# Four graph layers on one core: the comparison of a transposed block of adjacency comes two steps behind its transfer, with five buffers instead of four

## The chip, the cores and the metric

The kernel runs on one core of one Trainium2 chip. The metric is the device time of one execution in microseconds (us). The kernel before takes 3604.29 us, the median of three runs (3601.26 to 3607.97). The engines named below are TensorE (PE, with its weight loads as PEld), VectorE (DVE), ScalarE (ACT), GpSimd (POOL) and SyncE (SP), whose queue only issues transfers here.

## What is computed

Four layers run over 3327 nodes with 512 features; `adj` is a dense 3327 x 3327 matrix of int32 zeros and ones, shared by all layers. Layers 0, 1 and 2 are graph attention with 8, 4 and 8 heads, layer 3 is a mean over neighbours. Layer 0, cut to what matters:

```python
h = jnp.maximum(_layernorm(x, axis=-1), 0.0)
Wh = jnp.einsum('nd,hdo->hno', h, W)
e = jax.nn.leaky_relu(f1[:, :, None] + f2[:, None, :], negative_slope=ALPHA)
e = jnp.where(adj[None, :, :] > 0, e, NEG_INF)
attention = jax.nn.softmax(e, axis=-1)
h_prime = jnp.einsum('hnm,hmo->hno', attention, Wh)
x = x + elu(h_prime)
```

The product over neighbours wants adjacency with the neighbour on the partitions, so each 128 x 128 tile of `adj` must be transposed and turned into a mask of 0 and 2 in one-byte numbers.

## The kernel before

**Tiling.** The 3327 nodes are 26 tiles of 128. Rows are taken in 7 chunks of up to four tiles (`chunks`); columns in five groups of 6, 6, 6, 4 and 4 tiles (`JG`). `attention` (L678) runs over the chunks, within a chunk over the heads, within a head over two passes of two row tiles each. For every pair of row tile and column tile PE does two matmuls, one with `tht` (L760) and one with `gt` (L763). These two are made per column group by `matrices` (L646): four or six comparisons per group on ACT (L664) or DVE (L661), then on DVE an `and` with the mask (L668) and an `xor` (L670). There are seven buffers each of `tht` and `gt`, against five groups per head, so DVE and ACT can be little more than one group into the next head before PE has used the current one. At the end of a pass DVE sums the accumulators (`R`, L778), and at the end of a head it scales the result (L796 to L803).

**Where masks come from.** The masks of chunk 0 are made ahead of the loop with transposes on PE. Those of the other chunks are made during layer 0, 110 blocks (22 row tiles x 5 groups), by `mask_steps` (L212). Each block has three stages: `load` issues the transfer of `adj` to a tile `at` from POOL (L226; three buffers); `turn` issues from SP a transposing transfer of `at` into a tile `tr` (L238; four buffers); `compare` turns `tr` into `st` on DVE (L245), takes the diagonal tile where the block holds it (`d`, L250, and `dg`, L251; 22 blocks of the 110) and stores `st` to DRAM from SP (L252). `mask_tiles` (L261) loads the masks of a chunk back (L265).

**How the stages are staggered.** `in_steps` (L889) lays the blocks out as a pipeline: step `i` runs the last stage of block `i - s`, then the one before, down to the first stage of block `i`. With three stages there are 112 steps, and a comparison is in the step right after the one that issued its transposing transfer. `Hooks.run` (L602) is called after every pass (the "hook") and takes one step, or two on some hooks: on every odd one in chunk 0, and on every third in the chunks after it. So in a hook with two steps the transfer and its comparison can stand in the same hook. Before the last head of a chunk a loop (L808) takes further steps until the masks of the next chunk are done.

**What sets the order.** The program text is reordered by a scheduler, which puts each instruction on its engine's queue where it judges it ready; the queue itself is then in order. `after(inst, name)` holds an instruction behind a named one in that judgement: `load`, `turn` and the L245 comparison are held behind the last matmul of the pass (`gone[-1]`). `d` (L250) has no such hold.

The buffers of layer 0 are laid out by `tags` (L943): there `R` takes 4 x 2 x 129 floats per partition, while its layer-0 use is 4 x 2 x 65.

Of the kernel before, what the change touches and what calls it, by code (L numbers as in the profile page):

```python
# [25 lines left out]
F32 = mybir.dt.float32  # L26
BF16 = mybir.dt.bfloat16
# [10 lines left out]
P = 128  # L38
# [14 lines left out]
def tile_gnn(ctx: ExitStack, tc: tile.TileContext, x, adj, W0, a01, W1, al, ar, W2, a2,  # L53
# [7 lines left out]
    def pn(t):  # L61
        return min(P, N - t * P)

    PER = 4
# [3 lines left out]
    JM = max(n for _, n in JG)  # L68
# [76 lines left out]
    def after(inst, name):  # L145

        tc.add_manual_dep(inst.ins, name, mybir.DependencyInfo(mybir.DependencyClass.NoSync,
                                                               mybir.DependencyReason.SCHED_ONLY))
# [62 lines left out]
    def mask_steps(pool, t, g):  # L211


        n = pn(t)
        c, k = where[t]
        j0, nj = JG[g]
        w = min(nj * P, N - j0 * P)
        q = {}

        def load():  # L220
            at = q["at"] = pool.tile([P, JM * P], BF16, name="at", bufs=3)
            if n < P:
                nc.vector.memset(at, 0.0)
            elif w < nj * P:
                nc.vector.memset(at[:, w:nj * P], 0.0)
            ld = nc.gpsimd.dma_start(at[:n, :w], adj[t * P:t * P + n, j0 * P:j0 * P + w])  # L226
            after(ld, gone[-1] if gone else stored[NT - 1] if c else relus[-3])

        def turn():
            at = q["at"]  # L230
            if c == 0:
                tp = q["tp"] = ps.tile([P, 8, P], BF16, name="tp", bufs=2)
                for j in range(nj):
                    nc.tensor.transpose(tp[:, j, :], at[:, j * P:(j + 1) * P], identb)
                compare()
            else:
                tp = q["tp"] = mp.tile([P, JM, P], BF16, name="tr", bufs=4)
                tr = nc.sync.dma_start(tp[:, :nj], at[:, :nj * P], transpose=True)  # L238
                after(tr, gone[-1] if gone else stored[NT - 1])

        def compare():
            hooks.done += 1
            tp = q["tp"]
            st = masks0[g][:, k] if c == 0 else pool.tile([P, JM, P], FP8, name="st", bufs=3)[:, :nj]
            cm = nc.vector.tensor_scalar(st, tp[:, :nj], 0.0, 2.0, op0=ALU.is_gt, op1=ALU.mult, saturate=False)  # L245
            if gone:
                after(cm, gone[-1])
            if j0 <= t < j0 + nj:
                d = pool.tile([P, P], BF16, name="d", bufs=1)
                nc.vector.tensor_tensor(d, tp[:, t - j0, :], negI, ALU.is_gt)  # L250
                nc.vector.tensor_scalar(dg1[:, t, :], d, 2.0, None, op0=ALU.mult, saturate=False)  # L251
            nc.sync.dma_start(maskd[c][g][:, k], st)  # L252
        return (load, turn) if c == 0 else (load, turn, compare)

    def mask_view(c, g):
        nt, nj = chunks[c][1], JG[g][1]
# [635 lines left out]
    with tc.tile_pool(name="first", bufs=1) as fp:  # L892
# [21 lines left out]
        order = [(t, g) for g in range(len(JG)) for t in range(PER)]  # L914
        order += [(t, g) for t in range(PER, NT) for g in range(len(JG))]
        hooks.masks = in_steps([mask_steps(ip, t, g) for t, g in order[:20]])
        hooks.tiles = [node_stages(L, t, lambda lead=1, t=t: first_x(t, lead), fp, True) for t in range(NT)]
        folds, hooks.small = hooks.small, []
# [21 lines left out]
        while hooks.small:  # L940
            hooks.small.pop(0)()
    A, R = [("A", D, F32, n) for n in A_BUFS], ("R", PER * 2 * 129, F32, 1)
    ab, gt, tht = ("ab", JM * 400, BF16, 7), ("gt", PER * JM * P, FP8, 7), ("tht", PER * JM * P, FP8, 7)  # L943
    tags = [[A[0], R, tht, ("tr", JM * P, BF16, 4), ("abx", 4 * 400, BF16, 4), gt],
            [A[1], ("ab", JM * 258, F32R, 7), R, ("ts", 2 * JM * P, F32R, 3), ("tv", 2 * 4 * P, F32R, 2), tht[:3] + (10,)],
            [A[2], ab, ("R", PER * 2 * 65, F32, 1), tht, gt]]
    hooks.masks = in_steps([mask_steps(ip, t, g) for t, g in order[20:]])
    for l in range(3):
        att = ExitStack()
        if l == 2:  # L950
            yp = main.enter_context(tc.tile_pool(name="early", bufs=1, side="right", reuse_waits="tile"))
        mp = att.enter_context(tc.tile_pool(name=f"att{l}", bufs=1, reuse_waits="tile"))
# [526 lines left out]
```

## Time and profile before

| | before |
|---|---|
| median of three runs | 3604.29 us |
| the profiled execution's own time | 3600.56 us |
| its span, first to last instruction | 3598.7 us |
| mean granted TensorE clock | 0.986 |
| PE busy in the span | 3457.0 us (96%) |
| DVE busy | 2619.6 us (73%) |
| ACT busy | 2508.1 us (70%) |
| transposing transfers (L238) | 110, issued from 187.9 to 997.5 us, 5.4 us median from issue to landing (2.9 to 10.8) |
| L245 on `tr` | 110, from 196.7 to 1010.2 us, 550 ns median |
| L250 on `tr` | 22, from 197.2 to 1004.3 us, 291 ns median |

The blocks of this change are made between about 190 and 1010 us of the span. "Idle before" in a row of the timeline is how long an engine stood still ahead of the instruction, with the engine or transfer whose semaphore released it.

### The profile page before, as it was taken

How to read it: one execution, taken by the hardware profiler on the slowest of the kernel's cores; microseconds unless marked ns; L12 is line 12 of the kernel's file. 1: busy time of each engine (PE TensorE's matmuls, PEld its weight loads, DVE VectorE, ACT ScalarE, POOL GpSimd, SP SyncE). 2: the span in 40 equal slices, each digit the busy share in tenths (PEclk: the TensorE clock that was granted, in tenths of full speed). 3: DMA queues.
4: the chain of work that ended last, by engine and by line, in shares of the span. 5: the costliest groups of instructions: out<-in, count | busy, mean ns of one | idle time of the engine just before them, and what ended most of it. 6: DMA issues, size and time to landing. Idle time of an engine off the chain costs nothing. (4 is left out here: it accounts for less than half of the span.)

```text
span 3598.7 us, 77661 instructions
## 1 busy us (share of the span) xinstructions
PE 3457.0 (96%) x30751; PEld 3114.2 (87%) x30751; DVE 2619.6 (73%) x5227; ACT 2508.1 (70%) x4113; POOL 620.4 (17%) x858
## 2 busy tenths in 40 slices
PE   7888999999999999999999989999999999999998
PEld 6778999999999878888888869989898989877887
DVE  7777778888887779898888868877676767672221
ACT  5766787777787888888888767766676667572111
POOL 6600222111110211232223230101010101010000
PEclk9999999999999999999999999999999999999999
DMA  7698899999966877777777886655555555576331
GB/s 212 217 257 209 220 255 231 248 250 256 241 214 211 299 251 288 263 266 281 276 254 272 298 289 216 196 169 174 179 193 173 183 177 179 167 266 260 118 103 56
DMA packets 398120, 797.72 MB, mean 222 GB/s; under 512 B 112969, under 2 KB 221844, under 8 KB 397104
## 3 DMA queue, kind: packets, MB, share of 16 engines
q1 hardware_dynamic: 363890, 723.14, 62.6%
q0 software_dynamic: 28128, 62.42, 7.6%
q10 hardware_dynamic: 5726, 7.08, 0.6%
q8 instruction: 245, 4.01, 0.5%
q14 instruction: 131, 1.07, 0.1%
HBM read 663.59 MB, written 129.64 MB: 220 GB/s over the span
## 5 line engine op out<-in xcount | busy, mean ns | idle before, releaser
L664 ACT ACTIVATE gt<-s1b,ks 128x512 fp8e4<-128x512 f32 (+1 forms) x2448 | 1448.0, 677 | 291.5 <-issue 175.8
L760 PE MATMUL acc<-ab,tht 128*128 128x195 bf16 (+1 forms) x9112 | 1559.6, 249 | 10.1 <-DVE tht L668 9.3
L763 PE MATMUL acc<-ab,gt 128*128 128x195 bf16 (+1 forms) x9112 | 1558.5, 249 | 7.2 <-DVE gt L670 3.6
L763 PEld LDWEIGHTS <-gt 128*128 128x128 fp8e4 x10744 | 1056.4, 98 | 60.1 <-issue 44.4
L760 PEld LDWEIGHTS <-tht 128*128 128x128 fp8e4 x10744 | 1055.7, 98 | 41.8 <-DVE tht L668 28.1
L668 DVE TENSOR_TENSOR tht<-gt,m 128x768 uint32<-128x768 uint32 (+3 forms) x557 | 446.5, 802 | 118.4 <-ACT gt L664 116.8
L670 DVE TENSOR_TENSOR gt<-tht,m 128x768 uint32<-128x768 uint32 (+3 forms) x557 | 449.5, 807 | 8.7
L633 ACT CAST ts<-tht 128x1536 fp32r<-128x1536 fp8e4 x208 | 300.0, 1469 | 58.6 <-PE acc L753 54.9
L753 PE MATMUL acc<-ab,ts 128*128 128x258 f32 x2496 | 332.3, 289 | 5.5 <-DMA ab<-ab 3.4
L753 PEld LDWEIGHTS acc<-ab,ts 128*128 128x128 f32 x2496 | 312.0, 189 | 15.0 <-issue 3.7
L763 PE MATMUL acc<-abx,gt 128*128 128x195 bf16 (+1 forms) x1632 | 289.4, 250 | 27.1 <-DVE rc L800 15.4
L661 DVE TENSOR_SCALAR gt<-s1b,ns 128x512 fp8e4<-128x512 f32 (+1 forms) x446 | 216.0, 490 | 131.2 <-PE acc L763 130.4
L664 ACT ACTIVATE tht<-s1b,ks 128x512 fp8e4<-128x512 f32 (+1 forms) x504 | 308.3, 679 | 3.0 <-DMA s1b<-s 2.5
L1015 PE MATMUL acc<-y,mf 128*128 128x512 f32 x1352 | 309.8, 391 | 0.5 <-DVE mf L1010 0.5
L760 PE MATMUL acc<-abx,tht 128*128 128x195 bf16 (+1 forms) x1632 | 290.2, 250 | 14.4 <-DVE tht L668 11.3
L1015 PEld LDWEIGHTS acc<-y,mf 128*128 128x128 f32 x1352 | 253.5, 188 | 56.6 <-DVE mf L1010 0.9
L863 POOL TENSOR_TENSOR xt<-xt,e 128x512 f32<-128x512 f32 x72 | 126.1, 1752 | 913.8 <-DVE e L862 595.5
L778 DVE TENSOR_REDUCE R<-acc 128x130 f32<-128x390 f32 x416 | 214.5, 555 | 77.5 <-PE acc L763 76.8
L756 PE MATMUL acc<-ab,tht 128*128 128x387 bf16 x1248 | 227.3, 331 | 8.5 <-DMA ab<-ab 4.7
L1012 ACT CAST mf<-m 128x768 fp32r<-128x768 fp8e4 (+1 forms) x78 | 59.1, 762 | 243.9 <-PE acc L1015 232.1
L753 PE MATMUL acc<-ab,tv 128*128 128x258 f32 x1664 | 219.1, 283 | 2.3 <-DVE tv L633 1.5
L753 PEld LDWEIGHTS acc<-ab,tv 128*128 128x128 f32 x1664 | 207.1, 189 | 4.3 <-DVE tv L633 2.7
(163 smaller groups left out, 3709.1 us busy)
## 6 DMA issues: line engine op xcount, KB each, us to landing
ab<-ab SPq DMA_DIRECT2D x333, 600.0 KB, 5.3
ab<-ab SPq DMA_DIRECT2D x112, 774.0 KB, 6.4
ab<-ab SPq DMA_DIRECT2D x112, 516.0 KB, 5.4
ab<-ab SPq DMA_DIRECT2D x112, 400.0 KB, 3.9
abx<-ab SPq DMA_DIRECT2D x110, 400.0 KB, 7.3
ab<-ab SPq DMA_DIRECT2D x56, 582.0 KB, 7.1
s1b<-s SPq DMA_DIRECT2D x120, 256.0 KB, 6.1
m<-mask SPq DMA_DIRECT2D x69, 384.0 KB, 4.1
```

The costliest lines, as they stand in the source:

```text
L633: (nc.scalar.copy if KIND[g] == "s" else nc.vector.tensor_copy)(t[:, :k1 - k0, :nj], th[a][g][:, k0:k1])
L661: nc.vector.tensor_scalar(gv[:, :, jj, :], s1v, L.ns2[:, j, h:h + 1], 2.0, op0=ALU.is_gt, op1=ALU.mult, saturate=False)
L664: nc.scalar.activation(gv[:, :, jj, :], s1v, AF.Relu, bias=L.ks2[:, j, h:h + 1], scale=BIG, saturate=False)
L668: nc.vector.tensor_tensor(pu, gu, mu, ALU.bitwise_and)
L670: nc.vector.tensor_tensor(gu, pu, mu, ALU.bitwise_xor)
L753: mm = nc.tensor.matmul(acc[k][:, :2 * DA], thr[g][:, k - ks[0], jj, :], ab[a][g][:, jj, :], start=(j == 0), stop=(j == NT - 1), skip_grou ...
L756: mm = nc.tensor.matmul(acc[k][:, :3 * DA], th[a][g][:, k, jj, :], ab[a][g][:, jj, :3 * DA], start=(j == 0), stop=(j == NT - 1), skip_grou ...
L760: nc.tensor.matmul(acc[k][:, :3 * DA + o], th[0][g][:, k, jj, :], ab[0][g][:, jj, :3 * DA + o], start=(j == 0), stop=False, skip_group_che ...
L763: mm = nc.tensor.matmul(acc[k][:, AO:AO + 3 * DA + o], th[1][g][:, k, jj, :], ab[0][g][:, jj, AO:AO + 3 * DA + o], start=False, stop=(j == ...
L778: nc.vector.tensor_reduce(R[:, k], v.rearrange("p a (s d) -> p a d s", s=3), AX.X, ALU.add)
L863: nc.gpsimd.tensor_add(xt, xt, e)
L1015: nc.tensor.matmul(acc[k], mf[:, jj, :], y2[g][:, jj, s, :], start=(j0 + jj == 0 and s == 0), stop=(j0 + jj == NT - 1 and s == 1))
```

## The change

A fourth stage that does nothing is put between `turn` and `compare`, so a comparison comes two steps behind the issue of its transposing transfer; there are 113 steps instead of 112. `tr` gets a fifth buffer (1536 bytes per partition), and the reservation of `R` in layer 0 shrinks from 129 to 65 floats (2048 bytes per partition less). No instruction is added or removed.

```diff
-                tp = q["tp"] = mp.tile([P, JM, P], BF16, name="tr", bufs=4)
+                tp = q["tp"] = mp.tile([P, JM, P], BF16, name="tr", bufs=5)
                 tr = nc.sync.dma_start(tp[:, :nj], at[:, :nj * P], transpose=True)
...
-        return (load, turn) if c == 0 else (load, turn, compare)
+
+        return (load, turn) if c == 0 else (load, turn, lambda: None, compare)
...
-    tags = [[A[0], R, tht, ("tr", JM * P, BF16, 4), ("abx", 4 * 400, BF16, 4), gt],
+    tags = [[A[0], ("R", PER * 2 * 65, F32, 1), tht, ("tr", JM * P, BF16, 5), ("abx", 4 * 400, BF16, 4), gt],
```

## The prediction, made before the changed kernel ran

> **What bounds the kernel now.** I began with the page: PE is busy for 96% of the span, so time is won only where PE stands still or is slow. Busy time by stretch then shows where that is, for the stage in which masks are made:
>
> ```profile
> 190.00:340.00 150.00, 128.85 (x1409) 124.40 (x1410) 113.42 (x233) 102.54 (x168) 12.52 (x23) 0.94 0.94 232
> 340.00:600.00 260.00, 243.24 (x2645) 236.85 (x2643) 204.07 (x414) 199.97 (x339) 58.73 (x83) 0.96 0.93 226
> 600.00:1010.00 410.00, 398.03 (x4388) 388.86 (x4386) 334.14 (x703) 321.90 (x547) 68.18 (x102) 1.00 1.00 255
> ```
>
> The columns are the stretch, its length, busy us (and instructions) of PE, PEld, DVE, ACT and POOL, then the granted TensorE clock, the DMA share and GB/s. PE is idle for 21.2 + 16.8 + 12.0 = 49.9 us of these 820 us. It also runs at a reduced clock: 0.06 x 150 + 0.04 x 260 = 19 us of full clock are missing. DVE is busy for 651.6 us (79%), so on average it has room. The list of waits, cut to 180 to 1015 us, says who stops it:
>
> ```profile
> DVE st L245 <- DMA tr<-at: 75.7, 26, 7.7
> DVE d L250 <- DMA tr<-at: 38.7, 14, 6.6
> DVE tht L668 <- ACT gt L664: 24.1, 29, 2.5
> ...
> PE acc L760 <- DVE tht L668: 17.2, 15, 3.1
> PE acc L763 <- DVE rc L800: 15.4, 11, 6.4
> PE acc L763 <- DVE gt L670: 8.9, 8, 2.4
> PE acc L763 <- DVE rc L801: 4.8, 3, 3.7
> PE acc L760 <- DMA mask<-st: 3.1, 1, 3.1
> ```
>
> (Total us, times, longest.) DVE stands 114.4 us for transposed blocks that have not landed; PE stands for DVE. The timeline joins the two:
>
> ```profile
> 390.57 0.68 DVE L668 TENSOR_TENSOR tht<-gt,m 128x512 uint32<-128x512 uint32 x1
> 391.17 0.69 DVE L796 TENSOR_TENSOR R<-R,cpm 128x520 f32<-128x520 f32 x1
> ...
> 396.89 0.43 DVE L245 TENSOR_SCALAR st<-tr 128x512 fp8e4<-128x512 bf16 x1 [5.02 <-DMA tr<-at]
> 397.23 0.42 DVE L798 TENSOR_TENSOR R<-R 128x260 f32<-128x260 f32 x1
> 397.57 0.69 DVE L670 TENSOR_TENSOR gt<-tht,m 128x512 uint32<-128x512 uint32 x1
> 398.17 0.16 DVE L800 TENSOR_SCALAR rc<-R 128x4 f32<-128x4 f32 x1
> 398.25 0.95 DVE L668 TENSOR_TENSOR tht<-gt,m 128x768 uint32<-128x768 uint32 x1
> 398.40 0.32 PE L763 MATMUL acc<-abx,gt 128*128 128x195 bf16 x1 [6.40 <-DVE rc L800]
> ```
>
> The head's last `gt` (L670) stands behind the comparison. The comparison is held 5.02 us by its transfer, and PE, whose next matmul needs that `gt`, stands 6.40 us. (The releaser named is `rc`; the missing operand is the `gt` that ends just then.)
>
> **What the Trainium skill says.** "Perfetto Trace Analysis", Tensor Engine Instruction, calls ACT, DVE and GpSimd strict FIFO; the rows above agree, L798 and L670 start only once L245 has. "DMA: Bandwidth & Descriptors", Rules for kernel authors, says to issue a transfer early, compute, and wait for its semaphore late, which is the form of this change. "TensorE: Matmul & The Clock Gate", Part 1, says the clock halves after an idle window of about 3.4 us and returns after about 3.4 us of work. Here it agrees: the 10 us from 394, from 536 and from 327 us were granted 0.66, which is 6.8 us at half rate each.
>
> **The change, part by part.** (1) *The waits of L245.* I set each idle stretch of PE over 0.25 us between 180 and 1015 us beside DVE's last wait before it in the timeline: 42 stretches, 52.6 us. About 37 us follow a wait of L245 for `tr`; 5.5 us follow such a wait at 327 us, where the loop at L808 takes extra steps; 4.6 us follow a wait of L250; 4.0 us are the first passes before 194 us; 1.5 us have no such cause. One pass is about 10 us (19.7 us per head), and one step more puts at least one pass between the issue of a transfer and its comparison, where the two now can share a hook. Landing takes 5.4 us in the median and 10.8 at most, so nearly all of the 26 waits go. Not all of PE's 37 us go with them: the stretches of 0.4 to 0.8 us at head ends stand behind DVE's own chain of sums. I take 30 us.
>
> (2) *The clock.* Half-rate stretches follow L245 waits at 266, 352, 394 (two), 588 and 896 us: with grants of 0.83, 0.83, 0.66, 0.83 and 0.83 over 10 us that is 1.7 + 1.7 + 3.4 + 1.7 + 1.7 = 10.2 us of clock. PE stood still in part of it. I take 9 us.
>
> (3) *The diagonal `d`.* The order of the built kernel shows what the text doesn't: `d` is not held behind the pass, so the scheduler still puts it where it thinks the transfer has landed, and that does not move by a step. Before, 17 of the 22 `d` stand ahead of their L245; after, all 22 do, by 10 to 33 instructions. So the 14 waits (38.7 us) stay and up to 8 come new, each like those there are, 2.8 us: some 22 us more of DVE standing. What that costs PE is small as long as DVE is ahead: of the 14 waits only three are followed by idle PE, 4.6 us in all, plus 3.4 us of clock at 536 us; that is 0.6 us per `d`. Eight more are 5 us. If none of the new ones is felt it is 0; at the size of the one at 536 us (2.9 us idle and 3.4 of clock) all eight would be 50 us.
>
> (4) *The loop at L808, and the queues.* At the end of chunk 0 the loop takes two steps instead of one, so the comparisons of blocks 18 and 19 still stand in the same hook as the issue of their transfers: the 5.5 us and 3.4 us of clock at 327 us stay. On SP, the load of chunk 1's second mask group now stands behind the store of block 18 and two more transposes, where before it was issued at 315.7 us; by the DVE order it is wanted at about 332 us. With the store at about 328 us and 4.1 us for a mask load it comes 0 to 2 us late. With one more comparison of 0.55 us in that hook I take 1.5 us. Later chunks need no extra steps (42 blocks are compared by the step where 40 are needed).
>
> (5) *The rest.* SP's transposes stay one step behind the loads, so POOL's wait for `at` (234.2 us on `tr`) is as before and hides behind its idle time. Five `tr` buffers leave the same three steps of reuse as four did. The order of matmuls differs only within the first head, and the order after 1010 us not at all. `R` and `tr` shift addresses; I put that at 0, with 3 us either way for a wait at the start of layer 1 (2.8 us of PE at 1350 us now).
>
> DMA share is 0.93 to 1.00 in this stage, but in 940 to 1020 us PE was busy throughout beside a share of about 1, so a PE without gaps can be fed.
>
> Sum: 30 + 9 - 5 - 1.5 = 32.5, so the profiled time goes from 3600.56 to 3568. The runs' median lies 3.7 us above the profiled time, which gives 3571.8; I say 3571.
>
> **The rivals.** *A, the sum above:* 3571, own range 3548 to 3590. The upper end is (1) and (2) in full, the 8.9 us of (4) won too and no `d` felt anew: 37 + 10.2 + 8.9 = 56 us; the lower one is 14 us, a third of (1) and (2).
>
> *B, the wait moves to `d`.* DVE still stands for `tr`, in 22 places instead of 40, and these come where it is just in time. For it: the order of the built kernel. Against it: eleven of the 14 waits at `d` cost PE nothing. If half of the gain is given back, 3604 - 16 = 3588.
>
> *C, nothing shows:* transfers are the true limit, the blocks land later as PE gets faster, and the gaps return at `ab` or the masks. For it: the share of 1.00. Against it: PE waits for a transfer once in the stage, 3.1 us. 3604, within 0.2%.
>
> *D, slower:* the same place as B at full price. `d` stands between `tht` and `gt` of a group, and all 22 hold the group that PE wants next. At 6 us of waiting with 2.5 us felt and 1.2 us of clock, 22 x 3.7 = 81, less the 8 there are now, against 39 + 1.5 won or lost elsewhere: 3604 + 73 - 37.5 = 3640. The point from which it decides is 2.1 us felt per `d`: (37.5 + 8) / 22. Mildly past it, at 2.6 us, 3616.
>
> **How the numbers follow.** A 0.62, B 0.15, C 0.08, D 0.15. A run of this kernel can be told from no change at about 0.2%, 7 us. Faster is A and B and a little of C: 0.78; same 0.07; slower 0.15. The range that leaves 2 in 10 out reaches from A's upper savings through B to just below no change: 3546 to 3598.
>
> **What would show it.** Waits of L245 for `tr` fall from 75.7 us to under 15; those of L250 stay or rise to 40 to 70 us; PE's idle time in the stage falls from 50 us to about 20; the grant rises to 0.97 or more in 190 to 340 us; the stage ends near 977 us instead of 1010, with nothing changed behind it. The wait at the end of chunk 0 (327 us, earlier by what is won before it) stays. Wrong would be: idle time of PE behind L250 as large as what L245 gave up, or PE waiting for masks or `ab`.

## The result, and the profile after

The changed kernel takes 3561.08 us, the median of four runs (3554.17 to 3569.33), beside 3605.22 us for the kernel before (four runs). The ratio is 0.9879, 95% interval 0.9855 to 0.9903, so it is faster by 35 to 52 us, 1.2%. The profiled execution took 3569.33 us (the slowest of the four) with a span of 3567.4 us, 31.3 us less than before; the kernel before was profiled at 3600.56 us, under its own median. From L254 on, the line numbers of the changed kernel are one higher: L669 is the `and` (L668 before), L671 the `xor`, L761 and L764 the matmuls, L801 and L802 the `rc` rows.

Busy time by stretch, changed kernel, with the columns of before (length, then busy us of PE, PEld, DVE, ACT, POOL, granted clock, DMA share, GB/s):

```profile
190.00:340.00 150.00, 142.32 (x1606) 140.16 (x1607) 125.71 (x259) 113.55 (x185) 16.50 (x29) 0.95 1.02 255
340.00:600.00 260.00, 249.36 (x2731) 243.10 (x2729) 212.04 (x426) 206.92 (x352) 61.98 (x86) 0.98 0.99 239
600.00:980.00 380.00, 373.37 (x4132) 365.94 (x4130) 317.86 (x663) 303.20 (x516) 62.99 (x95) 1.00 1.01 257
```

PE's idle time in the stage is 7.7 + 10.6 + 6.6 = 24.9 us where it was 49.9, and the missing clock 0.05 x 150 + 0.02 x 260 = 12.7 us where it was 19.4. That is 32 us together. The instructions of the stage are the same; in its first 150 us PE got through 1606 matmuls instead of 1409.

The list of waits of the changed kernel, 180 to 985 us (total us, times, longest):

```profile
DVE d L250 <- DMA tr<-at: 53.1, 17, 7.7
DVE tht L669 <- ACT gt L665: 34.4, 40, 2.5
...
DVE tht L669 <- DMA tr<-at: 5.3, 1, 5.3
DVE st L245 <- DMA tr<-at: 3.9, 1, 3.9
...
DVE tht L669 <- DMA m<-mask: 2.2, 1, 2.2
...
PE acc L761 <- DVE tht L669: 16.2, 10, 3.2
PE acc L764 <- DVE gt L671: 4.2, 4, 1.4
PE acc L764 <- DVE rc L801: 3.8, 5, 0.8
```

The comparison L245 waits once instead of 26 times. `d` waits more than before (53.1 us, it was 38.7), and 40 short waits for ACT instead of 29 fit a DVE that is less often late and now meets operands that ACT has not made yet. All instructions on the blocks, as the view of one tile gives them:

```profile
L238 SPq DMA_TRANSPOSE tr<-at x110: 1188/1274/3857, 184.9 to 958.8; - x110
L245 DVE TENSOR_SCALAR st<-tr x110: 392/551/1631, 202.2 to 977.6; 128x768 fp8e4<-128x768 bf16 x66, 128x512 fp8e4<-128x512 bf16 x44
...
DMA to landing us min/median/max: 2.4/5.2/10.7
```

The transfers are as slow to land as before (5.2 us in the median, 5.4 before); they are only waited for later. The last comparison starts at 977.6 us instead of 1010.2, and from there to the end of the span it is 2589.8 us, where it was 2588.5. Everything won in this profile is won in this stage.

### The profile page after: what moved, and what is told of

Same layout as the page of the kernel before. It is cut to its first block, busy times and chain, and to the rows that moved or that the text cites. A ratio compares the mean times of both kernels' runs of the same rounds, so it can differ in the third digit from the quotient of the medians.

```text
span 3567.4 us, 77669 instructions
## 1 busy us (share of the span) xinstructions
PE 3450.4 (97%) x30751; PEld 3112.8 (87%) x30751; DVE 2626.8 (74%) x5227; ACT 2507.5 (70%) x4113; POOL 626.2 (18%) x858
## 5 line engine op out<-in xcount | busy, mean ns | idle before, releaser
L761 PE MATMUL acc<-ab,tht 128*128 128x195 bf16 (+1 forms) x9112 | 1556.3, 248 | 6.1 <-DVE tht L669 5.3
L764 PE MATMUL acc<-ab,gt 128*128 128x195 bf16 (+1 forms) x9112 | 1555.2, 248 | 5.8 <-DVE rc L801 3.3
L764 PEld LDWEIGHTS <-gt 128*128 128x128 fp8e4 x10744 | 1055.2, 98 | 38.1 <-issue 25.8
L761 PEld LDWEIGHTS <-tht 128*128 128x128 fp8e4 x10744 | 1054.6, 98 | 36.9 <-DVE tht L669 23.3
L669 DVE TENSOR_TENSOR tht<-gt,m 128x768 uint32<-128x768 uint32 (+3 forms) x557 | 448.1, 805 | 136.9 <-ACT gt L665 127.7
L671 DVE TENSOR_TENSOR gt<-tht,m 128x768 uint32<-128x768 uint32 (+3 forms) x557 | 449.9, 808 | 8.5
L761 PE MATMUL acc<-abx,tht 128*128 128x195 bf16 (+1 forms) x1632 | 289.0, 250 | 15.0 <-DVE tht L669 14.8
L764 PE MATMUL acc<-abx,gt 128*128 128x195 bf16 (+1 forms) x1632 | 288.5, 250 | 8.4 <-DVE rc L801 3.8
```

Of the source, the lines that this page charges most:

```text
L669: nc.vector.tensor_tensor(pu, gu, mu, ALU.bitwise_and)
L671: nc.vector.tensor_tensor(gu, pu, mu, ALU.bitwise_xor)
L761: nc.tensor.matmul(acc[k][:, :3 * DA + o], th[0][g][:, k, jj, :], ab[0][g][:, jj, :3 * DA + o], start=(j == 0), stop=False, skip_group_che ...
L764: mm = nc.tensor.matmul(acc[k][:, AO:AO + 3 * DA + o], th[1][g][:, k, jj, :], ab[0][g][:, jj, AO:AO + 3 * DA + o], start=False, stop=(j == ...
```

## The experiments

Each ratio is to the kernel before, run on the same chip as the experiment. Times in us of different sets are not compared directly: the kernel before has medians of 3605.22, 3599.46, 3596.66 and 3598.05 us in the four sets.

### Which part of the change does it: e1 and e2

e1 has the empty stage alone, e2 the buffers alone.

```diff
 e1
-        return (load, turn) if c == 0 else (load, turn, compare)
+        return (load, turn) if c == 0 else (load, turn, lambda: None, compare)
 e2
-                tp = q["tp"] = mp.tile([P, JM, P], BF16, name="tr", bufs=4)
+                tp = q["tp"] = mp.tile([P, JM, P], BF16, name="tr", bufs=5)
...
-    tags = [[A[0], R, tht, ("tr", JM * P, BF16, 4),
+    tags = [[A[0], ("R", PER * 2 * 65, F32, 1), tht, ("tr", JM * P, BF16, 5),
```

> The empty stage alone: four buffers for tr, R reserved as before. Its instructions stand in the same order on every engine as in the changed kernel. Theory (the step of distance makes the gain): as the changed kernel, 3553 to 3570 us, waits of L245 for tr under 10 us, idle PE of the mask stage near 29 us; a fourth buffer that is held a step longer can cost up to 5 us by transposes that wait for DVE. Rival (the fifth buffer or the smaller R makes it): 3600 to 3610 us with L245 waiting some 70 us as before.

> The fifth buffer and the smaller R alone, the comparison one step behind as before; its instructions stand in the order of the kernel before. Theory: no change, 3598 to 3612 us, waits of L245 for tr about 76 us. Rival (buffers): 3555 to 3570 us.

e1: 3560.5 us, ratio 0.9889 (0.9868 to 0.9910). e2: 3600.5 us, ratio 1.0004 (0.9992 to 1.0016). Who waited for the tile `tr`, in e1 first, then in e2:

```profile
  DVE d L250: 52.6, 15
  DVE st L245: 4.4, 1
```

```profile
  DVE st L245: 79.3, 24
  DVE d L250: 39.3, 14
```

The empty stage is the whole effect, as far as these runs can tell. The fifth buffer and the smaller `R` alone change nothing beyond 0.16%, and on top of the stage their effect is within the intervals (0.9889 beside 0.9879): four buffers held a step longer showed no cost, although the expectation left up to 5 us for it.

### More and less distance: e4 and e7

```diff
 e4 (from before)
-        return (load, turn) if c == 0 else (load, turn, compare)
+        return (load, turn) if c == 0 else (load, lambda: (turn(), compare()))
 e7 (from the changed kernel, six buffers for tr)
-        return (load, turn) if c == 0 else (load, turn, lambda: None, compare)
+        return (load, turn) if c == 0 else (load, turn, lambda: None, lambda: None, compare)
```

> From the kernel before, the other way: the comparison in the same step as the issue of its transfer, so that all 110 can meet a transfer that has not landed (5.4 us in the median). Theory (DVE's waits for tr reach PE nearly in full once its room is used): DVE's waits for tr grow from 114 us to 300 to 550 us and the time to 3700 to 3950 us. Rival (PE hides most of them): under 3640 us.

> The comparison three steps behind, six buffers for tr, d not held. Theory (two steps already outlast the landing, L245 waits only 4 us): no further gain, 3556 to 3570 us, ratio 0.987 to 0.991, waits at d as in the changed kernel. Rival (more distance wins more): under 3552 us.

e4: 3639.64 us, ratio 1.0107 (1.0084 to 1.0129). e7: 3553.48 us, ratio 0.9881 (0.9866 to 0.9896). The direction of e4 is as expected, the size is not: 40 us are lost where 100 to 350 were expected. Its time is under the rival's figure (3640 us) by 0.4 us. In the view of `tr`, e4 shows why:

```profile
  DVE st L245: 167.4, 71
...
DMA to landing us min/median/max: 2.8/5.9/9.8
```

DVE's waits are 167 us, not 300 or more: 39 of the 110 comparisons found their block landed, and the others waited 2.4 us each beside a landing time of 5.9. Those 39 start 6.3 us after the issue of their transfer in the median, so other work of DVE stands between the two even within one step. So a step of distance is not the only cover a transfer has. The rival's reason, that PE hides most of the waiting, is not borne out: DVE waits 53 us more than in the kernel before (167.4 and 114.4 us), and the time grows by 40. PE's idle time from 190 us to the last comparison is 77.0 us, where it was 49.9. In ratio, from the same step to three steps behind, the times are 1.0107, 1, 0.9876 to 0.9889, and 0.9881: the third step adds nothing. (e7's time in us is a little under the range expected, and the kernel before is 9 us faster on its chip than in the first set; the ratio is in its range.) There was only one wait of L245 for `tr` left to take, 3.9 us at the end of chunk 0. It is gone, but L245 now waits for something else in the same place, as the list of waits and the timeline of e7 show:

```profile
DVE st L245 <- DMA mask<-st: 5.0, 2, 4.3
...
311.18 0.43 DVE L245 TENSOR_SCALAR st<-tr 128x512 fp8e4<-128x512 bf16 x1 [4.29 <-DMA mask<-st]
```

That is the three buffers of `st`, which must be stored before the comparison can reuse them. From 300 to 330 us PE is idle for 5.5 us in e7 and for 4.1 us in the changed kernel, so nothing was won there. A wait at `d` of 4.67 us follows in e7 at 318 us, and the trace does not tell what each of the two costs.

### What d costs: e3 and e6

```diff
-                nc.vector.tensor_tensor(d, tp[:, t - j0, :], negI, ALU.is_gt)
+                dd = nc.vector.tensor_tensor(d, tp[:, t - j0, :], negI, ALU.is_gt)
+                if gone:
+                    after(dd, gone[-1])
```

e3 has this in the changed kernel, e6 in the kernel before.

> The changed kernel with d (L250) also held behind the last matmul of the pass. Theory (the 53 us that DVE still stands at d are felt by PE at about 17 us): waits at d fall under 10 us, idle PE of the mask stage from 29 to about 12 us, 10 to 22 us faster than the changed kernel: 3539 to 3551 us. Rival (d stands where DVE is ahead and its waits are free): waits at d fall too, but the time stays at 3556 to 3568 us.

> The kernel before, comparison one step behind, with d held. Theory (the distance is what counts, holding d helps only once L245 finds its block landed): d's waits of 39 us go, but L245 itself waits 80 to 110 us for tr; 3592 to 3606 us, ratio 0.997 to 1.001. Rival (d was the costly wait all along): 3580 to 3590 us, ratio under 0.996.

e3: 3551.11 us, ratio 0.9866 (0.9847 to 0.9886). e1 has the order of the changed kernel and ran on the same chip: its four runs took 3555.71 to 3565.95 us, those of e3 3548.93 to 3553.11 us. The medians are 9.4 us apart, just under the 10 to 22 expected, though the intervals of the ratios overlap. The waits at `d` are gone. PE's idle time from 190 to 980 us is 18.9 us, where it is 25.5 in e1; 12 was expected. Waits in another place have come in for those at `d`, as in e11 further down, which is e3 once more:

```profile
DVE at L225 <- DMA tr<-at: 12.4, 4, 3.8
...
DVE at L223 <- DMA tr<-at: 5.6, 3, 2.3
```

At the edges of the matrix, `load` clears a part of a new tile `at` on DVE (L223, L225), and that has to wait until the transposing transfer of the tile's last user has read it. This is 18.0 us in e11 and 20.8 us in e3, where the same view gives 0.7 us in the kernel before and 2.1 us in the changed one. So part of what holding `d` takes from DVE's waits comes back in this form. What that part costs PE is not shown.

e6: 3587.28 us, ratio 0.9973 (0.9962 to 0.9984, 22 runs). That lies in the range of ratios expected, near its lower end; the time in us lies in the rival's range, but the kernel before is also faster on this chip (3596.66 us), so the ratio decides. All 22 `d` now come after their comparison and wait no more, and the waits of L245 stand where they were, not higher as expected. From the list of waits of e6 (L670 is the `and`, L672 the `xor`, L762 and L765 the matmuls, L802 the first `rc` row):

```profile
DVE st L245 <- DMA tr<-at: 76.1, 26, 6.6
...
PE acc L762 <- DVE tht L670: 18.0, 11, 4.1
PE acc L765 <- DVE rc L802: 9.0, 7, 4.5
PE acc L765 <- DVE gt L672: 7.4, 6, 1.9
```

From 190 us to the last comparison PE is idle for 36.3 us, against 49.9 us in the kernel before and 52.0 in e2, which has the same order. These are single profiles, and that of e6 is the fastest of its 22 runs (3574.41 us). The medians say that the 39 us of waits at `d` cost the kernel before 9.4 us, 6 to 14 by the interval; that they are free, as the expectation had it, is not so.

### The end of chunk 0, and the best version: e5, and the set on one chip

```diff
-                        hooks.run(1 if last else 3, hook, 2 if hook % 2 and c == 0 or hook % 3 == 0 and c else 1, 2 if last else 1)
+                        hooks.run(1 if last else 3, hook, 2 if (hook % 2 or hook in (8, 12)) and c == 0 or hook % 3 == 0 and c else 1, 2 if last else 1)
```

This is on top of the held `d`. Chunk 0 has taken all its steps by hook 13, so the loop at L808 takes none, and blocks 18 and 19 are compared one hook after their transfers are issued.

> The changed kernel with d held, and with two steps instead of one on hooks 8 and 12 of chunk 0, so that the loop at L808 has no step left to take. Theory (blocks 18 and 19 are compared in the hook that issues their transfers, 4 us of idle PE and 6.8 us at half clock in e3): the wait of L245 at about 313 us goes, 4 to 9 us under e3, ratio to the kernel before 0.984 to 0.9855. Rival (the stall is one of the masks of chunk 1 and stays): the ratio of e3, 0.9866.

> The changed kernel once more, on the chip of the three runs beside it. It has the order of e1, so theory: 3553 to 3568 us, waits at d 45 to 60 us, idle PE of the mask stage 24 to 32 us. Rival (its first figure was high or low by chance): more than 8 us off 3561.

e5: 3544.37 us, ratio 0.9843 (0.9824 to 0.9861). e9: 3551.8 us, ratio 0.9876 (0.9862 to 0.9891); its time in us is 9 under the first figure, but so is the kernel before on that chip, and the ratio is the same. e5 is in the range of ratios expected. Because e3 and e5 had been on different chips, the two and the changed kernel were put on one:

> The changed kernel beside e11 and e12 on one chip, since e3 and e5 were each measured on another one than it. Ratio to the kernel before 0.987 to 0.989.

> The changed kernel with d held, as e3. Theory (waits at d reach PE even with the longer distance, 8 to 15 us): 7 to 14 us under e10. Rival (the difference of e3 was one between chips): within 4 us of e10.

> The changed kernel with d held and two steps on hooks 8 and 12 of chunk 0, as e5. Theory: 4 to 9 us under e11. Rival (nothing but chance between e3 and e5): within 3 us of e11.

| on one chip | us | ratio to before (95%) |
|---|---|---|
| e10, the changed kernel | 3552.24 | 0.9876 (0.9856 to 0.9897) |
| e11, and d held | 3548.01 | 0.9858 (0.9837 to 0.9879) |
| e12, and hooks 8 and 12 doubled | 3536.32 | 0.9834 (0.9815 to 0.9852) |

Holding `d` on top of the longer distance is 4 us here, between the 7 expected and the rival's limit, and its interval overlaps that of e10. With the 9.4 us between e1 and e3 it is likely that it gains, but on top of the change the size is not settled. The step of e12 is 11.7 us, more than the 4 to 9 expected; its interval overlaps e11's a little, and lies clear of e10's. The place can be read in the stretch from 300 to 330 us, in e11 first and then in e12:

```profile
300.00:330.00 30.00, 25.15 (x265) 24.38 (x264) 20.42 (x40) 18.80 (x31) 3.37 (x7) 0.89 1.01 230
```

```profile
300.00:330.00 30.00, 30.00 (x359) 30.00 (x358) 25.71 (x54) 22.93 (x38) 2.21 (x4) 1.00 1.09 267
```

PE's 4.9 us of idle time and 0.11 x 30 = 3.3 us of missing clock are gone there, 8.2 us in all. e12 is the fastest version found, 1.7% under the kernel before.

## Why the prediction was right, and which terms were mis-sized

**The sum.** It said 32.5 us off the profiled execution, and the two profiled executions differ by 31.2 us; the stage ended at 977.6 us, where 977 was said. That it fits so closely is luck: the changed kernel's profiled run was its slowest. The medians differ by 44 us, and in e1, e9 and e10, which have the same order, by 39, 45 and 46 us. So the mechanism was right and the sum 6 to 13 us too low, with the result inside the range. PE's idle time tells the same: 24.9 us from 190 to 980 us in this profile, 25.5, 19.6 and 19.4 in those of e1, e9 and e10, where it was 49.9 before and about 20 was said.

**(1) The waits of L245.** Right: 75.7 us to 3.9 us, and e1 shows that the distance alone does it. Of the 37 us of PE's idle time that I set down to them, some may belong to `d`, see (3).

**(2) The clock.** Right in kind. The missing clock fell by 6.7 us in this profile, where 9 us less some for `d` were said. At 344 to 357 us and 430 to 440 us, waits at `d` still lead to idle PE, and the grant of 340 to 600 us is 0.98, not 1. What the prediction takes from the Trainium skill ("TensorE: Matmul & The Clock Gate", Part 1), that the clock halves after an idle window of about 3.4 us, agrees with the traces in the length of the slow stretches (a grant of 0.66 over 10 us is 6.8 us at half rate), but not always in the idle time that comes with them. At the three places named there, PE stood still for 6.40 us up to 398 us, but only for 3.11 and 2.42 us up to 329 and 331 us, and for 2.23 and 0.65 us up to 538 and 539 us.

**(3) The diagonal d.** The order of the built kernel was the right place to look: 22 `d` stand ahead of their comparison, 17 of them wait, 53.1 us in all (40 to 70 said). That is three waits and 14 us more than before, where up to 8 and 22 us were said. The price of a wait is less sure. I charged each idle stretch of PE to the last wait of DVE before it. The timeline of the changed kernel shows what this misses:

```profile
430.07 0.29 DVE L250 TENSOR_TENSOR d<-tr,negI 128x128 bf16<-128x128 bf16 x1 [6.28 <-DMA tr<-at]
...
435.93 1.03 DVE L779 TENSOR_REDUCE R<-acc 128x130 f32<-128x390 f32 x2
436.88 2.01 DVE L245 TENSOR_SCALAR st<-tr 128x768 fp8e4<-128x768 bf16 x2
438.81 0.69 DVE L797 TENSOR_TENSOR R<-R,cpm 128x520 f32<-128x520 f32 x1
...
439.43 0.68 DVE L669 TENSOR_TENSOR tht<-gt,m 128x512 uint32<-128x512 uint32 x1
...
440.16 0.35 PE L761 MATMUL acc<-abx,tht 128*128 128x195 bf16 x1 [3.21 <-DVE tht L669]
```

DVE stands 6.28 us at `d`, then works without a pause for ten microseconds, still late, and only then does PE run out. The two comparisons in between wait for nothing. In the kernel before such lateness would have been charged to a wait of L245 that came in between.

How much was mis-charged in all is open. For the kernel before, the prediction had 4.6 us of idle time and 3.4 us of clock, 8 us together; e6, without these waits, gained 9.4 us (6 to 14), so the sum was about right or somewhat low. In e6's one profile PE is idle 13.6 us less, but that is its fastest run. In the changed kernel, taking the waits at `d` away gained 9.4 us (e1 to e3) and 4 us (e10 to e11), no more than before, although new waits for `at` came in. So the 5 us that the sum took off for eight more `d` are not seen in the runs. In this profile 25.0 us of idle time and 6.7 us of clock were won, where the terms were 30 and 9, less 6.5 for (3) and (4). In the profiles of e9 and e10, which took 3554.87 and 3551.03 us, it was some 30 us of idle time and 10 and 11 us of clock: the two terms with nothing taken off. By these two profiles the mis-sized term is this deduction.

**(4) The end of chunk 0.** Right, the stall stays, by the timeline of the changed kernel:

```profile
311.08 0.43 DVE L245 TENSOR_SCALAR st<-tr 128x512 fp8e4<-128x512 bf16 x1 [3.93 <-DMA tr<-at]
...
312.50 0.26 PE L761 MATMUL acc<-abx,tht 128*128 128x195 bf16 x1 [2.67 <-DVE tht L669]
...
314.20 0.32 PE L764 MATMUL acc<-abx,gt 128*128 128x195 bf16 x1 [1.44 <-DVE gt L671]
```

This is the one wait that L245 has left. DVE also waits once, 2.2 us, for the second mask group of chunk 1, where up to 2 us were said. PE's idle time there is 2.67 + 1.44 = 4.1 us, where 5.5 were to stay.

**(5) The rest.** Right: e1 and e2 put the shifted addresses and the fifth buffer at nothing, and behind the stage the difference is 1.3 us. One thing was missed: DVE's waits for `at` (L223, L225) grow with the change as well, from 0.7 to 7.4 us. That counts the 5.3 us which the list of waits puts down to L669: neither of its operands comes by such a transfer, and the clearing of an `at` tile (L225) starts at the same moment, 541.47 us. With `d` held there are more of them (e3, e11).

**The rivals.** B's mechanism (the wait moves to `d`) is there, with about 14 us more waiting at `d` than before, but it gave back far less than half. C fell: the DMA share went to about 1 in the whole stage and PE still ran with half the idle time. (The 3.1 us for which PE was said to wait for a transfer in the kernel before are no such wait: that matmul starts at 328.75 us, and the `tht` that it reads was made by L668 on DVE from 328.00 us, for 0.69 us.) D's point was 2.1 us felt per `d`; all idle PE of the stage in the changed kernel, 24.9 us, and all its missing clock, 12.7 us, are 1.7 us per `d`, so it was not reached.

## What to carry to other kernels

An in-order engine that waits for a transfer delays everything queued behind it; the cure here was not a faster transfer but a consumer placed further behind, and one step was enough as soon as it outlasted the landing time. A consumer that no hold ties to its stage (here `d`) need not move when the stage is moved: look for it in the built order. Holding it as well is worth a try, but look for the wait that takes its place (`at` in e3 and e11, `st` in e7). When idle time of the bounding engine is charged to waits of its supplier, the last wait is not always the one at fault: after 430 us PE ran dry ten microseconds behind the wait that had made DVE late. A run without the waits in question puts a price on them, and its median, not its one profile, is the price.

## What the runs showed that I had not expected

A comparison in the same step as its transfer cost only 1.1%, as other work of DVE stands in between: 2.4 us waited per late block beside a landing of 5.9 us.

The DMA share is 0.99 to 1.02 throughout the changed stage, and e12 runs PE at 30.00 of 30 us with a share of 1.09. In these runs a share of 1 did not mean that transfers set the pace.
